# A gated cross-attention block on one core: reordering ScalarE's and GpSimd's work in the first attention group

## The chip, the cores and the metric

The kernel runs on one core of a Trainium2 chip. A core has five engines that each work through their own list of instructions in order: TensorE (PE in the profile, its weight loads PEld), VectorE (DVE), ScalarE (ACT), GpSimd (POOL) and SyncE (SP, which here issues most DMAs). An instruction that must wait for another engine's result holds up all that stands behind it in its own list. The metric is the time of one execution on the device in microseconds (us), as the median of several.

## The reference

The reference is a gated cross-attention layer followed by a gated linear layer, all in fp32:

```
x = x + tanh(g_xattn) * (softmax(q k^T / 8) v) Wo + bo     q = layernorm(x) Wq, k = ctx Wk, v = ctx Wv
x = x + tanh(g_ffn)   * (layernorm(x) W[idx] + b[idx])     idx = argmax(log_softmax(logits) + gumbel(u))
```

There are 4 batches of 2048 tokens with 512 features, 16 heads of 64, and 77 context tokens of 384 features for each batch.

## The kernel before

**Tiling.** The 8192 tokens go through in 16 groups of 512 (`T`, `NGRP`), four groups to a batch. The weights are folded first: a matrix `m` for each batch stands for Wq times that batch's keys, so that scores come from x in one product, and a matrix `vo` stands for values times Wo, so that the attention output comes from the probabilities in one product. `m` and `vo` are built once for all batches, stored to DRAM (`m_d`, `vo_d`), and one batch's part is loaded at a time (`load_m`, `load_vo`).

**Seven products.** Each big product (scores `ps_s`, attention `ps_a`, linear layer `ps_f`) is a two by two block product done with seven block products in place of eight. The class `Seven` (L445) holds this. It needs sums of weight blocks (`weight_sum`, L119, on POOL) and sums of column blocks called T1 to T4 (`Columns.sum`, L434, on POOL). `product(s)` issues the s-th block product on TensorE into one of three PSUM banks r; `post(s)` (L482) moves a result out: by ACT as a copy (`keep`, L472 or L476), or by DVE as an addition to what lies in SBUF already (L491). The order is a table (block, columns, bank r, starts a new bank):

```
ORDER = ((0, "B11", 0, True), (3, "T1", 1, True), (4, "T2", 0, False), (1, "B21", 2, True),
         (5, "T3", 0, False), (6, "B22", 1, False), (2, "T4", 0, False))
```

Blocks 0, 3, 4 and 2 are copied out by ACT, blocks 1, 5 and 6 are added by DVE. A product that goes on in a bank (False) must wait until the post before it has read that bank.

**Order of the work.** It is written out by hand: the program's order is each engine's order, and only the semaphores are put in for it. PSUM has seven banks for all products (`bank`, L82), handed out in turn as they come free.

**The stretch around the change** is the passage from set-up to the steady loop, group 0 (L738 to L800):

- `build_vo(p, engines)` (L327) makes the `vo` rows of the heads 2p and 2p+1. It takes six PSUM banks: for each of three row chunks one matmul for each of the two heads (L336). Each bank is scaled by the gate and copied to SBUF by DVE (L339) or ACT (L341), by the letters of `engines`, which repeat; then SP stores it (L345, L346).
- `head_max` (L527, DVE), `exps(i, n0, n1)` (L533, one ACT instruction for each of 64 pieces, 16 to a head), `head_sum` (L542, a sum and a reciprocal on DVE) and `head_scale` (L547, POOL) make the softmax of one group, head set by head set (four of them).
- `p_columns(i, k0, k1)` (L551) transposes key chunks k0 to k1 on DVE into the tile `pT`, from all four head sets at once. The attention product reads `pT`.
- In the loop at L747 the score products of group 1 (`s0`) alternate with the sets p = 4 to 7 of VO and with the exponentials of group 0. In the loop at L770 the remaining score products of group 1 (`s1` and `s2`) run while the last head sets are summed and scaled and the probabilities transposed; POOL makes T1 of `pT` and three of the four sums of VO (`weight_sum(vo, n)`: n = 0 makes block 5, n = 1 block 3, n = 2 block 4, n = 3 block 6). Then comes the steady loop over the groups (L802), which begins with the attention product `at` of group 0.

At the head of the program (L163 to L187) TensorE runs three matmuls on zeros, ACT and SP issue the first loads, and POOL writes the constants `neghalf` (-0.5) and `ones`. ACT's first computing instruction is then the copy of the first key projection (L275).

Of the kernel before, what the change touches and what calls it, by code (L numbers as in the profile page):

```python
# [8 lines left out]
F32 = mybir.dt.float32  # L9
U32 = mybir.dt.uint32  # L10
AF = mybir.ActivationFunctionType
# [3 lines left out]
P = 128  # L15
# [4 lines left out]
def flamingo_block_kernel(  # L20
# [33 lines left out]
    nc = tc.nc  # L54
    NT, D = x.shape
# [26 lines left out]
    small = ctx.enter_context(tc.tile_pool(name="small", bufs=2))  # L82
# [5 lines left out]
    def bank(name):  # L88
        return pm.tile([P, 512], F32, tag="mm", name=name)
# [8 lines left out]
    vo = cp.tile([P, 7, KH, D // 2], F32, tag="vo")  # L98
# [5 lines left out]
    neghalf = cp.tile([P, NG], F32, tag="neghalf")  # L104
# [9 lines left out]
    def flat(t):  # L114
        n = len(t.shape) - 1
        names = " ".join("abcdef"[:n])
        return t.rearrange(f"p {names} -> p ({names})")

    def weight_sum(w, n, engine=None):  # L119

        to, a, b_, op = ((5, 0, 3, ALU.subtract), (3, 3, 2, ALU.add), (4, 3, 0, ALU.subtract),
                         (6, 1, 4, ALU.subtract))[n]
        (engine or nc.gpsimd).tensor_tensor(flat(w[:, to]), flat(w[:, a]), flat(w[:, b_]), op)
# [19 lines left out]
    t = wp.tile([P, NK * T + KH * T2], F32, tag="pT", name="wq")  # L143
# [41 lines left out]

    nc.gpsimd.memset(neghalf, -0.5)
    nc.gpsimd.memset(ones, 1.0 / D)  # L187

    def by_chunk(t):

        return t.rearrange("p (a q e) -> p q a e", a=NA, e=32)

    def chunked(t):
        return t.rearrange("p (q a e) -> p q a e", a=NA, e=32)
# [61 lines left out]
    def v_cols(p, at, n):  # L256
        return vT_f[:, ds(p * BP + at, n)] if p < 7 else wf_f[:, ds(6 * D + at, n)]
# [65 lines left out]
    def stage_of(h):  # L323

        return vo_st[h if h < 2 else 2 + (h - 2) % (len(vo_st) - 2)]

    def build_vo(p, engines):  # L327
        n = 0
        for c in range(3):
            r = min(P, BP - c * P)  # L330
            for hh in range(2):
                stg = stage_of(2 * p + hh)
                hr = ts(hh, DH)
                ps = bank("ps_vo")

                nc.tensor.matmul(ps, v_cols(p, c * P, P)[hr], wo[hr, p, :], start=True, stop=True)  # L336
                src, dst = by_chunk(ps[:r, :]), chunked(stg[:r, c, :])
                if engines[n % len(engines)] == "D":
                    nc.vector.tensor_scalar(dst, src, tgx[:r], None, ALU.mult)  # L339
                else:  # L340
                    nc.scalar.activation(dst, src, AF.Copy, scale=tgx[:r])  # L341
                n += 1
        for hh in range(2):
            d, stg = vo_d[2 * p + hh], stage_of(2 * p + hh)
            nc.sync.dma_start(out=d[0 : 2 * P].rearrange("(c r) e -> r c e", r=P), in_=stg[:, 0:2])  # L345
            nc.sync.dma_start(out=d[2 * P :], in_=stg[: BP - 2 * P, 2])  # L346
# [5 lines left out]
    def load_vo(bi):  # L352
        src = vo_d.rearrange("h (r b k) e -> (h r) b k e", b=B, k=NK)[:, bi]
        for o, c in ((0, 0), (1, 0), (1, 1), (0, 1)):
            nc.sync.dma_start(out=vo[:, BLK[o, c]], in_=src[:, ts(c, KH), ts(o, D // 2)])
# [161 lines left out]
    def s_rows(i, k, cols):  # L517
        if i not in sc:
            sc[i] = wp.tile([P, HA, NG, JP], F32, tag="s", name="s")
        nc.vector.transpose(key_chunk(sc[i], k), cols.rearrange("p (g h r) -> p g h r", h=HA, r=R))  # L520

    def head(i, h):
        return sc[i][:, h, :, :J]
# [3 lines left out]
    def head_max(i, h):  # L527
        mx = stat[:, ds((16 + h) * NG, NG)]
        nc.vector.tensor_reduce(mx, head(i, h), AX.X, ALU.max)  # L529
        nmx[h] = small.tile([P, NG], F32, tag=f"nmx{h}", name="nmx")  # L530
        nc.vector.tensor_tensor(nmx[h], mx, norms[i].down, ALU.mult)  # L531

    def exps(i, n0, n1):  # L533

        for n in range(n0, n1):
            h, g = n // NG, n % NG
            nc.scalar.activation(head(i, h)[:, g, :], head(i, h)[:, g, :], AF.Exp,  # L537
                                 scale=norms[i].up[:, g : g + 1], bias=nmx[h][:, g : g + 1])
# [3 lines left out]
    def head_sum(i, h):  # L542
        sums[h] = sm = small.tile([P, NG], F32, tag=f"sm{h}", name="sm")
        nc.vector.tensor_reduce(sm, head(i, h), AX.X, ALU.add)  # L544
        nc.vector.reciprocal(sm, sm)  # L545

    def head_scale(i, h):  # L547
        nc.gpsimd.tensor_tensor(head(i, h), head(i, h), sums[h].unsqueeze(2).to_broadcast([P, NG, J]),  # L548
                                ALU.mult)

    def p_columns(i, k0, k1):  # L551
        for k in range(k0, k1):
            if k == 0:
                t = wp.tile([P, NK * T + KH * T2], F32, tag="pT", name="pT")
                pT[i] = Columns(t[:, : NK * T].rearrange("p (n t) -> p n t", t=T),
                                T1=t[:, NK * T :].rearrange("p (n t) -> p n t", t=T2))
            nc.vector.transpose(pT[i].all[:, k, :].rearrange("p (g h r) -> p g h r", h=HA, r=R),  # L557
                                key_chunk(sc[i], k))
# [103 lines left out]
    def centre_wf(wfr, c):  # L662
        nc.gpsimd.tensor_tensor(wfr[:, c, :], wfr[:, c, :], wf_mean, ALU.subtract)
        for o in range(2):
            nc.gpsimd.tensor_scalar(chunked(wf[:, BLK[o, c // 2], c % 2, :]), by_chunk(wfr[:, c, :])[:, ts(o, 2)],
                                    tgf, None, ALU.mult)
# [10 lines left out]
    def norm_step(n, s):  # L677
        if s == 0:
            n.gather()
        elif s == 1:  # L680
            n.calc()
            n.power()
        elif s == 2:
            n.back()
# [61 lines left out]
    e = (8, 16, 24, 32, 41, 50, 57)  # L746
    for s in range(6):  # L747
        s0.product(s)
        s0.post(s)
        if s < 2:  # L750
            centre_wf(wfr, 2 * s)
            centre_wf(wfr, 2 * s + 1)
        if s == 2:
            weight_sum(wf, 0)
            weight_sum(wf, 1)
        if s == 3:
            weight_sum(wf, 2)
        if s < 4:
            build_vo(4 + s, "DDA" if s < 2 else "D")
        if s < 2:  # L760
            head_max(0, 2 + s)
        exps(0, e[s], e[s + 1])
        if s == 3:
            weight_sum(wf, 3)
            load_vo(0)
        if 3 <= s:
            head_sum(0, s - 3)
            head_scale(0, s - 3)
    exps(0, 57, 64)
    for s in range(7):  # L770
        s1.product(s)
        s2.product(s)
        if s == 0:
            s1.post(0)
            s2.post(0)
            s0.product(6)
            s0.post(6)
            head_sum(0, 3)
            head_scale(0, 3)
        if s == 3:  # L780
            norm_step(n1, 2)
        if 1 <= s < 5:
            p_columns(0, (0, 2, 5, 7)[s - 1], (2, 5, 7, 10)[s - 1])
        if s == 2:
            pT[0].sum("T1")
        if s == 3:
            weight_sum(vo, 0)
        if s == 4:
            weight_sum(vo, 1)
        if s == 5:  # L790
            weight_sum(vo, 2)
            for k in range(4):
                s_rows(1, (0, 1, KH, KH + 1)[k], s0.chunk(k // 2, k % 2))
        if 0 < s:
            s1.post(s)
            s2.post(s)
# [5 lines left out]
    for i in range(1, NGRP):  # L802
# [69 lines left out]
        for s in range(7):  # L872
# [12 lines left out]
            if 1 <= s:  # L885
                e = (0, 10, 20, 32, 44, 56, 64)
# [121 lines left out]
    def by_feature(t, h, v):  # L1008

        return t[:, ts(v, NG // 2), ts(h, D // NA // 2)]  # L1010
# [24 lines left out]
    for s in range(6):  # L1035
# [23 lines left out]
        if s == 5:  # L1059
            f_rows(j, ff, 0, 0)  # L1060
            t = by_feature(ts_[j], 0, 0)
# [50 lines left out]
```

## Time and profile before

| what | value |
|---|---|
| time, median of 3 runs | 1245.52 us (1245.17 to 1245.72) |
| the profiled execution: time | 1246.03 us |
| its span in the trace | 1244.2 us |
| PE busy | 99% of the span, 5704 matmul passes |
| PEld busy | 85% |
| DVE busy | 73% |
| POOL busy | 72% |
| ACT busy | 55% |
| granted TensorE clock | 0.998 of full speed |
| share of the chain by `ps_s`, `ps_a`, `ps_f` | 39%, 37%, 15% |

An fp32 matmul shows as two passes, so counts of passes are twice those of matmuls. A line of the timeline has the start in us from the span's start, the length in us, the engine, the line of the program, the operation, the tile written and the tiles read, shapes, the count of instructions merged into the line, and in square brackets the idle time of the engine just before it with what ended it. A line of the chain has the start, the length, and what ran, with the number of merged instructions. A line of the waits has who waited for whom, the total in us, how often, and the longest.

### The profile page before, as it was taken

What the parts mean: (1) busy time and instruction counts of PE and PEld (TensorE: products, weight loads), DVE (VectorE), ACT (ScalarE), POOL (GpSimd) and SP (SyncE); (2) the same over time, 40 slices, a digit from 0 to 9 for tenths busy, and PEclk for the clock granted to TensorE, in tenths of its full rate; (3) what the DMA queues carried; (4) which work ended last, traced back from release to release, by engine and by line L of the source; (5) the groups of instructions that cost most, each with busy time, mean ns of one, the idle gap of its engine ahead of it and who ended that gap; (6) DMA issues with size and microseconds to landing.
All of it is one profiled execution on the core that took longest, in us unless ns stands there. A gap on an engine that the chain in (4) does not pass through costs nothing.

```text
span 1244.2 us, 16997 instructions
## 1 busy us (share of the span) xinstructions
PE 1234.0 (99%) x5704; PEld 1063.7 (85%) x5704; DVE 907.3 (73%) x1850; ACT 683.4 (55%) x1957; POOL 895.4 (72%) x486
## 2 busy tenths in 40 slices
PE   9999999999999999999999999999999999999997
PEld 6686888888888888888888888888888888888886
DVE  6778976666977766677776767776776877666576
ACT  4639545638274563827356382745638274563824
POOL 5558885857957785685968778575976877585766
PEclk9999999999999999999999999999999999999999
DMA  9868200314024030304106030212304121010102
GB/s 268 300 203 274 57 1 1 68 43 111 1 50 103 1 68 1 68 22 112 20 1 153 1 68 2 47 22 85 68 1 111 43 51 18 1 35 1 35 1 67
DMA packets 95221, 80.27 MB, mean 65 GB/s; under 512 B 3856, under 2 KB 83088, under 8 KB 95136
## 3 DMA queue, kind: packets, MB, share of 16 engines
q1 hardware_dynamic: 92496, 76.61, 24.1%
q10 hardware_dynamic: 2032, 1.47, 0.4%
q8 instruction: 45, 0.74, 0.3%
q0 software_dynamic: 608, 1.13, 0.2%
q14 instruction: 40, 0.33, 0.1%
HBM read 44.07 MB, written 35.13 MB: 64 GB/s over the span
## 4 chain that ended last, share of the span: by engine, by line
PE 96%; DVE 2%; ACT 0%; POOL 0%; issue 0%; DVEq 0%
PE ps_s L466 39%; PE ps_a L466 37%; PE ps_f L466 15%; PE ps_kv L270 2%; PE ps_vo L336 2%; PE ps_m L300 1%; DVE s L370 1%; PE ps_w L167 0%; ACT t L591 0%; POOL r L398 0%; DVE t L417 0%; DVE r L393 0%; DVE y L417 0%; DVE snap L491 0%; DVE y L587 0%
## 5 line engine op out<-in xcount | busy, mean ns | idle before, releaser
L466 PE MATMUL ps_a<-pT,vo 128*128 128x256 f32 x2240 | 486.2, 379 | 0.0
L466 PEld LDWEIGHTS ps_a<-pT,vo 128*128 128x128 f32 x2240 | 425.6, 190 | 57.9
L537 ACT ACTIVATE s<-s,nmx,up 128x77 f32<-128x77 f32 x1024 | 355.6, 445 | 0.8 <-DVE nmx L531 0.8
L437 POOL TENSOR_TENSOR pT<-pT 128x1280 f32<-128x1280 f32 x64 | 186.0, 2907 | 171.4 <-PE ps_a L466 161.9
L466 PE MATMUL ps_s<-tq,m 128*128 128x256 f32 x1280 | 290.6, 380 | 0.0
L466 PEld LDWEIGHTS ps_s<-tq,m 128*128 128x128 f32 x1280 | 242.6, 190 | 36.1 <-issue 2.3
L472 ACT COPY snap<-ps_s 128x512 f32<-128x512 f32 (+1 forms) x188 | 93.6, 515 | 292.7 <-DVE t L417 130.5
L466 PE MATMUL ps_s<-xc,m 128*128 128x256 f32 x960 | 221.1, 379 | 0.0
L466 PEld LDWEIGHTS ps_s<-xc,m 128*128 128x128 f32 x960 | 182.2, 190 | 27.3 <-issue 1.2
L548 POOL TENSOR_TENSOR s<-s,sm 128x1232 f32<-128x1232 f32 x64 | 145.2, 2271 | 46.7 <-DVE sm L545 46.7
L491 DVE TENSOR_TENSOR snap<-snap,ps_s 128x512 f32<-128x512 f32 (+1 forms) x141 | 83.7, 594 | 130.1 <-PE ps_s L466 125.0
L466 PE MATMUL ps_f<-tq,wf 128*128 128x256 f32 x512 | 118.3, 379 | 0.0
L557 DVE STREAM_TRANSPOSE pT<-s 128x512 f32<-128x512 f32 x160 | 101.0, 678 | 15.6 <-POOL s L548 15.6
L437 POOL TENSOR_TENSOR tq<-xc,tq 128x512 f32<-128x512 f32 x64 | 85.4, 1335 | 35.5 <-PE ps_f L466 33.0
L398 POOL TENSOR_TENSOR r<-r,neghalf 32x16 f32<-32x16 f32 (+1 forms) x33 | 93.2, 2833 | 21.9 <-DVE r L393 21.3
L466 PEld LDWEIGHTS ps_f<-tq,wf 128*128 128x128 f32 x512 | 97.3, 190 | 13.2
L544 DVE TENSOR_REDUCE sm<-s 128x16 f32<-128x1232 f32 x64 | 91.5, 1430 | 20.7 <-ACT s L537 20.7
L520 DVE STREAM_TRANSPOSE s<-snap 128x512 f32<-128x512 f32 x156 | 99.9, 685 | 6.1 <-ACT snap L472 3.8
L529 DVE TENSOR_REDUCE ps_st<-s 128x16 f32<-128x1232 f32 x64 | 92.4, 1444 | 2.1
L466 PE MATMUL ps_f<-xc,wf 128*128 128x256 f32 x384 | 90.7, 379 | 0.0
L437 POOL TENSOR_TENSOR tq<-xc 128x512 f32<-128x512 f32 x64 | 81.6, 1275 | 7.1 <-DVE xc L412 5.8
L472 ACT COPY snap<-ps_f 128x512 f32<-128x512 f32 x63 | 36.9, 586 | 87.8 <-PE ps_f L466 85.2
(138 smaller groups left out, 1187.0 us busy)
## 6 DMA issues: line engine op xcount, KB each, us to landing
xg<-in_x_dram SPq DMA_DIRECT2D x64, 256.0 KB, 6.0
out_dram<-y SPq DMA_DIRECT2D x60, 256.0 KB, 4.1
vo<-vo_d SPq DMA_DIRECT2D x16, 640.0 KB, 6.4
m<-m_d SPq DMA_DIRECT2D x12, 640.0 KB, 4.2
vo_d<-vo SPq DMA_DIRECT2D x14, 512.0 KB, 3.3
m_d<-vo SPq DMA_DIRECT2D x4, 960.0 KB, 5.0
wq<-in_WqT_dram SPq DMA_DIRECT2D x8, 256.0 KB, 6.5
wq<-in_Wo_dram SPq DMA_DIRECT2D x1, 2048.0 KB, 13.8
```

The source lines that it names most:

```text
L270: nc.tensor.matmul(ps[:, :n], w[:, c, ts(p, P)], keys[:, c].rearrange("p b j -> p (b j)"), start=(c == 0), stop=(c == NCC - 1))
L398: nc.gpsimd.tensor_tensor(r, r, neghalf[:32, : r.shape[1]], ALU.pow)
L437: (engine or nc.gpsimd).tensor_tensor(self.at[name], self.at[a], self.at[b_], op)
L466: nc.tensor.matmul(self.ps[r][:, n, :], self.w(blk, c, pair), self.cols(cname, c), start=(first and n == 0 and c == 0), stop=(c == h - 1), ...
L472: nc.scalar.copy(dst, self.ps[r])
L491: nc.vector.tensor_tensor(c, c, self.ps[r], ALU.add)
L520: nc.vector.transpose(key_chunk(sc[i], k), cols.rearrange("p (g h r) -> p g h r", h=HA, r=R))
L529: nc.vector.tensor_reduce(mx, head(i, h), AX.X, ALU.max)
L537: nc.scalar.activation(head(i, h)[:, g, :], head(i, h)[:, g, :], AF.Exp, scale=norms[i].up[:, g : g + 1], bias=nmx[h][:, g : g + 1])
L544: nc.vector.tensor_reduce(sm, head(i, h), AX.X, ALU.add)
L548: nc.gpsimd.tensor_tensor(head(i, h), head(i, h), sums[h].unsqueeze(2).to_broadcast([P, NG, J]), ALU.mult)
L557: nc.vector.transpose(pT[i].all[:, k, :].rearrange("p (g h r) -> p g h r", h=HA, r=R), key_chunk(sc[i], k))
```

## The change

Four edits, all in set-up and group 0:

1. After the constants are written, ACT computes one exponential of one column of `neghalf` into a small tile (tag `sm0`) that nothing reads.
2. For p = 6 and p = 7 (s = 2 and 3) the third of VO's six banks is copied by ACT rather than DVE ("DDADDD" for "D").
3. At s = 3 two of the exponentials are issued ahead of `build_vo(7)`, so that ACT's copy for p = 7 stands behind them. The last three exponentials (61 to 63) of group 0 are issued after the three copies that ACT makes in the first step of the next loop (`s1.post(0)`, `s2.post(0)`, `s0.post(6)`), not ahead of them.
4. `weight_sum(vo, 0)` on POOL moves from s = 3, behind T1 of `pT`, to s = 1, ahead of it.

ACT gains three instructions in all (1957 by the page before), DVE loses two, and POOL, PE and SP have as many as before. The table loads on ACT stay three, at the same three places in its list.

```diff
     nc.gpsimd.memset(neghalf, -0.5)
     nc.gpsimd.memset(ones, 1.0 / D)
+    t = small.tile([P, 1], F32, tag="sm0", name="sm")
+    nc.scalar.activation(t, neghalf[:, 0:1], AF.Exp)
...
+        e0 = e[s]
+        if s == 3:
+            exps(0, e0, e0 + 2)
+            e0 += 2
         if s < 4:
-            build_vo(4 + s, "DDA" if s < 2 else "D")
+            build_vo(4 + s, "DDA" if s < 2 else "DDADDD")
         if s < 2:
             head_max(0, 2 + s)
-        exps(0, e[s], e[s + 1])
+        exps(0, e0, e[s + 1])
         if s == 3:
             weight_sum(wf, 3)
             load_vo(0)
         if 3 <= s:
             head_sum(0, s - 3)
             head_scale(0, s - 3)
-    exps(0, 57, 64)
+    exps(0, 57, 61)
     for s in range(7):
         s1.product(s)
         s2.product(s)
...
             s0.product(6)
             s0.post(6)
+            exps(0, 61, 64)
             head_sum(0, 3)
             head_scale(0, 3)
+        if s == 1:
+            weight_sum(vo, 0)
         if s == 3:
             norm_step(n1, 2)
         if 1 <= s < 5:
             p_columns(0, (0, 2, 5, 7)[s - 1], (2, 5, 7, 10)[s - 1])
         if s == 2:
             pT[0].sum("T1")
-        if s == 3:
-            weight_sum(vo, 0)
         if s == 4:
             weight_sum(vo, 1)
```

## The prediction

> **What bounds the kernel now.** I read four views: the page, TensorE's waits, the chain, and the timeline from 85 to 140 us, the one stretch that the diff touches apart from the first instructions.
>
> The page, engines' busy time:
> ```profile
> PE 1234.0 (99%) x5704; PEld 1063.7 (85%) x5704; DVE 907.3 (73%) x1850; ACT 683.4 (55%) x1957; POOL 895.4 (72%) x486
> ```
> The waits of TensorE:
> ```profile
> PE ps_w L167 <- DVE tq L163: 1.5, 1, 1.5
> ```
> The chain, as start, length, what:
> ```profile
> 1.45 5.49 PE ps_w L167 x6
> ...
> 78.95 0.86 PE ps_w L659 x2
> ...
> 89.30 2.77 PE ps_vo L336 x12
> ...
> 98.70 3.02 PE ps_vo L336 x12
> ...
> 103.64 3.08 PE ps_vo L336 x12
> ...
> 108.64 3.02 PE ps_vo L336 x12
> 111.66 23.51 PE ps_s L466 x108
> ```
> PE is busy 1234.0 of 1244.2 us, and its only listed wait is the first instruction. In the stretch, the one loss that the chain shows is that the last three sets of VO banks (p = 5, 6, 7) take 3.02, 3.08 and 3.02 where an undisturbed one takes 2.77: 0.25 + 0.31 + 0.25 = 0.81 us. So a reordering can win at most that here, and it loses whatever idle time it opens on PE.
>
> The timeline, as start, length, engine, line:
> ```profile
> 101.68 1.27 ACT L341 ACTIVATE vo<-ps_vo,tg 128x512 f32<-128x512 f32 x2
> ...
> 102.84 2.86 ACT L537 ACTIVATE s<-s,nmx,up 128x77 f32<-128x77 f32 x8
> ...
> 105.57 0.59 ACT L472 COPY snap<-ps_s 128x512 f32<-128x512 f32 x1
> ...
> 106.04 13.83 ACT L537 ACTIVATE s<-s,nmx,up 128x77 f32<-128x77 f32 x40
> ...
> 109.74 4.03 DVE L339 TENSOR_SCALAR vo<-ps_vo,tg 128x512 f32<-128x512 f32 x6 [0.31 <-PE ps_vo L336]
> ...
> 115.53 8.95 POOL L548 TENSOR_TENSOR s<-s,sm 128x1232 f32<-128x1232 f32 x4 [2.45 <-DVE sm L545]
> ...
> 119.74 0.59 ACT L472 COPY sn<-ps_s 128x512 f32<-128x512 f32 x1
> ...
> 119.90 1.44 DVE L544 TENSOR_REDUCE sm<-s 128x16 f32<-128x1232 f32 x1 [0.16 <-ACT s L537]
> 120.21 0.88 ACT L472 COPY snap<-ps_s 128x256 f32<-128x256 f32 x2
> 121.37 0.25 DVE L545 RECIPROCAL sm<-sm 128x16 f32<-128x16 f32 x1
> ...
> 124.51 4.27 DVE L557 STREAM_TRANSPOSE pT<-s 128x512 f32<-128x512 f32 x7 [2.89 <-POOL s L548]
> ...
> 127.68 2.92 POOL L437 TENSOR_TENSOR pT<-pT 128x1280 f32<-128x1280 f32 x1 [3.20 <-DVE pT L557]
> ...
> 131.41 0.65 DVE L491 TENSOR_TENSOR sn<-sn,ps_s 128x512 f32<-128x512 f32 x1
> ...
> 132.42 2.75 PE L466 MATMUL ps_s<-tq,m 128*128 128x256 f32 x12
> ```
> Here is a second chain, a hair behind PE. ACT runs 40 exponentials without a pause from 106.04; the last ends at 119.87 and releases DVE's last row sum (119.90), its reciprocal (to 121.62), POOL's fourth head_scale (to 124.48), and DVE's ten transposes into pT (from 124.51). Behind those in DVE's queue stands s1.post(4), the addition at 131.41, which ends at 132.06. By the order table, s1.product(6) ("T4", bank 0) accumulates into the bank that s1.post(4) ("22", bank 0) reads, so it must wait for it. PE starts it at 132.42. The slack of the whole chain is 0.36 us.
>
> **The change part by part.**
>
> *Head exponential.* One ACT instruction of about 0.2 us after the first table load (2.21 to 3.49). Its input, POOL's memset at 0.80, is long written. ACT then idles until 8.59, 5.09 us waiting for PE: that is the cover. The instruction listing has three table loads before and after, so none is saved or added. Cost 0; were there one more load (1.28), the cover would still hold it. The page "ScalarE: Activation LUTs", section "What ACT_TABLE_LOAD costs", adds a drain of 1.38 us to a load, 2.66 in all; this trace shows only the 1.28, and the sum is 0 either way.
>
> *Two banks from DVE to ACT (third of six, p = 6 and 7).* DVE sheds two copies of 4.03/6 = 0.67. That gives PE nothing: the sixth matmul of a set waits for the bank that the first copy (still DVE's, at the same time) gives back, so 3.08 and 3.02 stay. Bounds: 0 to a win of 0.31 + 0.25 = 0.56; I take 0. SP's stores of these two sets and the vo load behind them (117.43) can only leave earlier. ACT's full queue takes the two copies, at (102.84 - 101.68)/2 = 0.58 each.
>
> ACT anew: the first copy runs at 106.04; ten exponentials at 13.70/40 = 0.343 each end at about 110.05. The second copy needs its bank of p = 7: the first bank is ready at 109.74 (DVE waited 0.31 for it), the next pair one PE step later, 2.77/3 = 0.92 at most, so at about 110.6. ACT waits 0.55 (bounds 0 and 0.61). Then copy, 27 exponentials (9.25), and the queue reaches the snap copies at 120.45 instead of 119.74.
>
> *Last three exponentials behind three copies.* The copies take 119.74 to 121.09, 1.2 us of queue (0.12 overlaps what follows). So the last exponential ends later by 0.58 + 0.58 + 0.55 + 1.2 = 2.9 us: at 122.8, not 119.87. Queued behind it: nothing that PE needs soon. The copies themselves are 0.7 late, but s1.product(2), which needs the first, starts at 122.05 (132.42 less 48 passes of 0.216, the pace of 28.49 us for 132 in a later stage of the chain) against its end at 121.05: hidden.
>
> *Down the second chain.* Sum and reciprocal take 119.90 to 121.62 = 1.72: done at 124.55. POOL's fourth head_scale used to wait for POOL itself until 122.2, so 0.4 of the delay is absorbed; it now starts 0.15 after the reciprocal (115.53 against 115.40 at the first) and ends at 126.97. The transposes start at 127.0 instead of 124.51: 2.5 late, on a DVE that idles meanwhile and is then full. s1.post(4) ends 7.55 later (132.06 - 124.51): 134.55.
>
> *VO's first sum ahead of T1.* One POOL instruction of 2.9 us goes in front of T1, in the 3.20 us that POOL idles there. Its vo blocks were loaded from 117.43 and land some 6.4 later (median of these loads), before 126.97. It ends at 129.95, T1's inputs (five transposes, 0.6 each) are there at 130.0, so T1 is not held up; the other two sums end at about 139.4 instead of 139.88. No cost, and no PE wait was there to win.
>
> *Sum.* s1.product(6) can start at 134.55 plus hand-over and an unhidden weight load. Bounds for that: 0.05 and 0.05 + 0.22; I take 0.15. So 134.7 against 132.42: PE idles 2.3 us. Everything behind it is gapless PE work, so 2.3 reaches the end. The rest of DVE's and ACT's queue (head_max, the next exponentials) is 2.5 late against a PE that is 2.3 late; the next consumer, the fifth attend product, had 2.7 us in hand (ACT's copy before it ended at 149.55, and PE, 80 passes of 0.216 after 135.01, reached it at 152.3). Bounds of the sum: 1.7 (no wait for the bank, the shortest restart) and 2.9 (copies at their full 0.69 and 1.35, the longest restart).
>
> The profiled execution took 1246.03 (span 1244.2 and 1.8 around it), 0.5 above the median 1245.52. In its terms the changed kernel takes 1248.3; against the median, 1245.52 + 2.3 = **1247.8 us**.
>
> **The clock.** Right after the start six ps_w passes take 5.49 us (0.92 each); at 78.95 two of the same shape take 0.86 (0.43 each): TensorE starts at about half speed, and those first 5.3 us cost 5.49 - 6 x 0.43 = 2.9. No row shows an idle PE of 2.3 us in mid-run, so a second slow spell is bounded by 0 and 2.9; I take 0, since PE never stood still that long after the start. The page "TensorE: Matmul & The Clock Gate", section "Why this matters for your kernels", sets the limit at idle gaps of about 3 us; by it the sum stays 2.3, and a gap past it would make it about 5.2.
>
> **Rivals.**
> 1. *Not slower: the second chain does not reach PE.* It decides at 124.87, the latest start of the transposes that keeps 0.36 of slack. For it: PE waits nowhere now. Against: ACT has no idle time between 101 and 121, so 2.9 of added queue can't vanish. Were it hidden, and the 0.56 won, 1245.0 to 1245.5.
> 2. *Slower by more than 2.5: the idle gap costs clock as well.* 2.3 plus up to 2.9: 1248.5 to 1250.7. For it: the slow start. Against: no such row in mid-run.
> 3. *A second late wait:* the delay breaks another slack, first the fifth attend product, which waits for ACT's copy behind twenty exponentials. Price up to 1 us: 1248.8. Against: 2.7 us in hand and only 0.2 of relative delay.
> 4. *The change does what it seems meant to:* ACT's copies earlier, PE's split pairs closed, 1245.0. Against: the copies come later, not earlier.
>
> **How the numbers follow.** My forecast 80%, rivals 1 and 4 together 9%, rival 2 6%, rival 3 5%. The forecast's own range is 1247.2 to 1248.4; the range that holds 8 in 10 widens it by half a microsecond below and above for the spread of runs (1245.17 to 1245.72) and for rival 3: 1246.5 to 1249.0. A difference of 0.2% (2.5 us) is about what a measurement of this kernel can tell from none; that line lies at 1248.0, inside my bounds: some three tenths of the forecast's 80%, and rivals 2 and 3, lie past it. So slower 0.36, same 0.62; faster by 2.5 us would need gains that PE's 0.81 us do not hold: 0.02.
>
> **What would show it.** In the changed profile TensorE's waits list a second line, ps_s on DVE's sn addition, of about 2.3 us near 132; the last exponential ends near 122.8, the transposes start near 127.0, ps_vo of p = 6 and 7 still takes 3.08 and 3.02, and PE is gapless from there on. I am wrong if PE shows no such wait, if the transposes start before 124.9, or if the clock row drops after the gap.

## The result, and the profile after

| what | before | after |
|---|---|---|
| time, median of 11 runs each | 1245.52 us (1244.76 to 1246.36) | 1248.53 us (1247.80 to 1249.42) |
| the profiled execution: time | 1246.03 us | 1249.04 us |
| its span | 1244.2 us | 1247.3 us |
| idle time of PE in mid-run | none | 2.00 us, once |

The ratio of the medians is 1.0024, with a 95% interval from 1.0016 to 1.0032. The kernel became slower by 3.0 us. The prediction said 1247.8 us, in a range from 1246.5 to 1249.0.

In these pages the profiled execution of the changed kernel runs 0.92 us ahead of the one of before from the first products on: its six `ps_w` passes at the start take 4.41 us where they took 5.49. This differs from one execution to the next of the same program: in three profiles of the changed kernel these passes take 4.41, 4.56 and 5.15 us. So the edits are not taken to be its cause, and 0.92 is added below wherever a time of after is held against one of before or of the prediction. Line numbers of after are two higher than before's up to L760.

The page of the changed kernel, engines' busy time:

```profile
PE 1235.0 (99%) x5704; PEld 1064.3 (85%) x5704; DVE 905.9 (73%) x1848; ACT 684.5 (55%) x1960; POOL 894.8 (72%) x486
```

It hardly differs: DVE gave up two instructions, ACT got three, and PE does the same passes in 1.0 us more of busy time. The shares tell nothing of what happened. The waits of TensorE in the changed kernel (who waited for whom, total in us, how often, longest):

```profile
PE ps_s L468 <- DVE sn L493: 2.0, 1, 2.0
PE ps_w L167 <- DVE tq L163: 1.5, 1, 1.5
```

The second line is the old one. The first is new, and it is the only wait that the change put into PE's list of 5704 passes. The chain of the changed kernel, in the stretch from 95 to 140 us, shows what it waits for (start, length, what):

```profile
107.73 1.97 PE ps_vo L338 x8
109.69 0.67 ACT vo L343
110.36 6.68 ACT s L539 x20
...
117.11 2.50 ACT s L539 x7
119.61 0.47 ACT sn L474
120.07 0.75 ACT snap L474 x2
120.82 1.05 ACT s L539 x3
...
121.89 1.45 DVE sm L546
...
123.36 0.26 DVE sm L547
...
123.77 2.27 POOL s L550
...
126.06 2.21 DVE pT L559 x4
...
133.04 0.58 DVE sn L493
...
133.67 4.54 PE ps_s L468 x12
138.21 1.94 PE ps_a L468 x9
```

Before, the chain went through PE alone here. Now it leaves PE at 109.7, when the matmul for a bank of p = 7 releases ACT's copy of it. It follows ACT's exponentials, the three copies that now stand in front of the last three, the row sum and reciprocal, the fourth `head_scale` and the transposes, and it comes back to PE at 133.67 with `s1.product(6)`. Every piece that the prediction called the second chain is in it.

The last lines hold a second thing. The twelve passes of `s1.product(6)` take 4.54 us where before they took 2.75. The stretches of the changed kernel show why (from and to, length, then busy us and number of instructions of PE, PEld, DVE, ACT and POOL, the granted TensorE clock as a share of full speed, the DMA share and GB/s):

```profile
4.65:131.67 127.02, 127.02 (x593) 91.42 (x591) 97.38 (x240) 74.37 (x213) 82.24 (x64) 1.00 0.87 263
131.67:133.67 2.00, 0.00 (x1) 0.00 (x1) 2.00 (x5) 0.00 (x0) 2.00 (x4) 1.00 0.00 0
133.67:134.36 0.69, 0.69 (x3) 0.64 (x4) 0.69 (x2) 0.00 (x0) 0.69 (x1) 1.00 0.00 0
134.36:137.77 3.41, 3.41 (x10) 2.70 (x9) 3.41 (x7) 0.58 (x1) 3.33 (x2) 0.50 0.00 0
137.77:150.00 12.23, 12.23 (x58) 10.75 (x58) 11.89 (x19) 7.74 (x22) 8.04 (x4) 1.00 0.00 1
```

PE stands still from 131.67 to 133.67 while DVE and POOL are busy throughout. It then works for 0.69 us at full clock, and at 134.36 the granted clock falls to 0.50 for 3.41 us. The attention product starts at these times in the changed kernel, in before, and in a second execution of the changed kernel that has no drop of the clock (below):

```profile
138.05 7.29 PE L468 MATMUL ps_a<-pT,vo 128*128 128x256 f32 x33
```

```profile
135.01 30.38 PE L466 MATMUL ps_a<-pT,vo 128*128 128x256 f32 x140
```

```profile
136.88 8.37 PE L468 MATMUL ps_a<-pT,vo 128*128 128x256 f32 x38
```

The stretch between two starts, of `s1.product(6)` and of the attention product, is 138.05 - 133.67 = 4.38 us here and was 135.01 - 132.42 = 2.59. Of the 1.79 more, 0.10 is the restart (the execution without the drop takes 134.19 to 136.88, which is 2.69), and 1.69 is the clock.

The sum of the profiled execution: 0.92 gained at the start; 2.17 lost in the gap, as `s1.product(6)` starts at 133.67 + 0.92 = 134.59 in place of 132.42 (the wait is listed with 2.00, since the pass before it still counts as busy for the other 0.17); 0.10 lost by the restart; 1.69 lost by the clock. Together it is 3.04 us later. The spans differ by 1247.27 - 1244.25 = 3.02. Nothing else moved the end.

### The profile page after: what moved, and what is told of

It is laid out like the page before. It is cut to its first block, busy times and chain, and to the rows that moved or that the text cites. A ratio compares the mean times of both kernels' runs of the same rounds, so it can differ in the third digit from the quotient of the medians.

```text
span 1247.3 us, 16995 instructions
## 1 busy us (share of the span) xinstructions
PE 1235.0 (99%) x5704; PEld 1064.3 (85%) x5704; DVE 905.9 (73%) x1848; ACT 684.5 (55%) x1960; POOL 894.8 (72%) x486
## 4 chain that ended last, share of the span: by engine, by line
PE 94%; DVE 3%; ACT 1%; POOL 0%; issue 0%; DVEq 0%; POOLq 0%
PE ps_s L468 37%; PE ps_a L468 37%; PE ps_f L468 15%; PE ps_kv L272 2%; PE ps_vo L338 2%; PE ps_m L302 1%; ACT s L539 1%; DVE s L372 1%; DVE pT L559 0%; ACT t L593 0%; PE ps_w L167 0%; POOL r L400 0%; DVE snap L493 0%; DVE t L419 0%; DVE r L395 0%
```

## Experiments

Four theories of the parts were put up before the runs: that the second chain, made late by edits 2 and 3 (the banks and the split), causes the gap; that only one of them does; that the head exponential or VO's sum has a part in it; and, on the clock, that a gap of this kind lowers it afterwards. The diffs below are against the changed kernel unless said otherwise.

### The split undone

```
-    exps(0, 57, 61)
+    exps(0, 57, 64)
...
-            exps(0, 61, 64)
```

> The changed kernel with the last three exponentials back in front of ScalarE's three copies; the head exponential, the two banks on ScalarE and VO's first sum stay. Theory A (the second chain: last exponential, row sum, head_scale, transposes, s1.post(4), s1.product(6)): ScalarE's delay is 0.58 + 0.58 + 0.45 = 1.6 us, less 0.4 of slack on GpSimd and 0.36 before TensorE, plus 0.15 to restart: an idle gap of 0.8 to 1.1 us, the clock stays at 1.00, 1246.3 to 1246.7 us. Theory B (the two banks on ScalarE do no harm, the split alone does all of it): no gap, 1245.5. Theory C (any idle gap of TensorE costs one 3.41 us spell at half clock, 1.7 us): 1248.2.

Measured: 1247.06 us (1246.04 to 1247.56), against 1245.51 for before on the same chip, ratio 1.0011 (1.0002 to 1.002). The wait of TensorE and the copy from which ACT's queue can be timed, in this kernel:

```profile
PE ps_s L468 <- DVE sn L493: 0.7, 1, 0.7
```

```profile
110.43 0.69 ACT L343 ACTIVATE vo<-ps_vo,tg 128x512 f32<-128x512 f32 x1 [0.39 <-PE ps_vo L338]
111.02 10.40 ACT L539 ACTIVATE s<-s,nmx,up 128x77 f32<-128x77 f32 x30
```

The last exponential now ends 121.42 - 110.43 = 10.99 us after the start of that copy; in the changed kernel it is 121.86 - 109.68 = 12.18. So the split is worth 1.19 us of lateness; the prediction had 1.2. Of the gap 0.66 is left (0.93 with the restart and the end of the pass before), and the clock stays at 1.00 after it. So the gap doesn't come from the split alone.

### The two banks given back to DVE

```
-            build_vo(4 + s, "DDA" if s < 2 else "DDADDD")
+            build_vo(4 + s, "DDA" if s < 2 else "D")
```

> The changed kernel with the six banks of p = 6 and 7 all on VectorE again; the split of the last exponentials and the rest stay. Theory A: ScalarE's delay is 1.2 us, less 0.4 and 0.36, plus 0.15: a gap of 0.5 to 0.7 us, clock 1.00, 1246.0 to 1246.3 us. Theory B turned round (the banks alone do it): no gap, 1245.5. Theory C: 0.6 and 1.7 more, 1247.8.

Measured: 1246.64 us (1245.69 to 1247.27), ratio 1.0007 (0.9998 to 1.0016). The wait:

```profile
PE ps_s L468 <- DVE sn L493: 0.5, 1, 0.5
```

Each edit alone costs PE less than a microsecond (0.93 and, here, 0.79, in both with the restart and the end of the pass before), and both together 2.27. The lateness of the last exponential adds up, nearly, and the loss does not. ACT's copy that starts at 105.57 in before starts at 105.42 with the banks alone, 105.33 with the split alone and 104.65 with both. Moved by these differences, the last exponential ends 1.70, 1.41 and 2.91 us after the 119.87 of before. Taking off the prediction's slack of 0.36 and its 0.4 of absorption on POOL, and putting on 0.10 for the restart, gives 1.04, 0.75 and 2.25. The slack of the one chain is spent once, and the second edit pays nearly in full. Both edits make the gap.

The times of both runs lie above the ranges expected, and 0.3 to 0.6 above before plus the time lost in the gap of their profile. Of the 0.6 of the split undone, 0.15 has a row: the 32 passes of score products that start at 117.74 in before take 7.07 us there, and 7.22 here, where ACT's first copy ends only at 121.89. The rest is within the intervals and left as unexplained.

### Only the head exponential and VO's sum

Against before, this kernel has the new exponential at the head and VO's first sum ahead of T1, and nothing else of the change.

```
+    t = small.tile([P, 1], F32, tag="sm0", name="sm")
+    nc.scalar.activation(t, neghalf[:, 0:1], AF.Exp)
...
+        if s == 1:
+            weight_sum(vo, 0)
...
-        if s == 3:
-            weight_sum(vo, 0)
```

> The kernel before with only the head exponential and VO's first sum ahead of T1. Theory A: neither touches a chain that TensorE waits on: no gap, 1245.5 us within 0.3. Rival D (the head exponential shifts the start of the program, or the sum on GpSimd slows the transposes beside it): some 0.3 to 1 us either way, and a transposes row longer than 4.27 us for seven.

Measured: 1245.90 us (1245.13 to 1246.50), ratio 1.0001 (0.9992 to 1.001). TensorE's only wait is the old one at the start. The timeline of this kernel:

```profile
3.51 0.20 ACT L189 ACTIVATE sm<-neghalf 128x1 f32<-128x1 f32 x1
8.06 0.42 ACT L277 COPY wf<-ps_kv 128x308 f32<-128x308 f32 x1 [4.34 <-PE ps_kv L272]
...
123.92 2.91 POOL L123 TENSOR_TENSOR vo<-vo 128x1280 f32<-128x1280 f32 x1
...
127.16 2.92 POOL L439 TENSOR_TENSOR pT<-pT 128x1280 f32<-128x1280 f32 x1 [0.33 <-DVE pT L559]
```

The exponential takes 0.20 us, and ACT idles 4.34 us behind it for PE. VO's sum runs in the time in which POOL waited for the transposes, and T1 still waits for DVE (0.33), not for the sum. The seven transposes beside VO's sum take 4.27 us, as in before, so rival D has no row for it. Two edits of the four open no wait. The median lies 0.4 above before, 0.1 more than was expected, and the interval holds zero: neither a cost nor a win can be told.

### The two posts issued ahead of the transposes

If the gap comes from the order of DVE's queue, where `s1.post(4)` stands behind transposes that start late, it must vanish when the posts of s = 3 and 4 are issued first.

```
+        if 3 <= s < 5:
+            s1.post(s)
+            s2.post(s)
         if 1 <= s < 5:
-            p_columns(0, (0, 2, 5, 7)[s - 1], (2, 5, 7, 10)[s - 1])
+            p_columns(0, (0, 2, 5, 5)[s - 1], (2, 5, 5, 10)[s - 1])
...
-        if 0 < s:
+        if 0 < s and s not in (3, 4):
             s1.post(s)
             s2.post(s)
```

> The changed kernel in full, but VectorE takes the posts of s = 3 and s = 4 (s1.post(3), s2.post(3), s1.post(4), s2.post(4)) ahead of the transposes of key chunks 5 to 9. ScalarE's late exponentials stay, so the transposes still start near 126. Theory A (the wait is made by VectorE's queue order): s1.post(4) ends near 130, TensorE has no wait at s1.product(6), no slow spell, 1245.5 us within 0.4. Rival E (the late transposes themselves hold up the attention product that reads them): a gap at the first ps_a products instead, 1246.5 or more.

Measured: 1247.60 us (1246.71 to 1248.15), ratio 1.0014 (1.0005 to 1.0023). The wait at `s1.product(6)` is gone, as expected, but the time of before does not come back, against the 1245.5 expected. The transposes start as late as in the changed kernel (127.17, with a start of this execution that is 0.15 later than before's, against 126.06 + 0.92 = 126.98), and `s1.post(4)` now stands ahead of the second half of them:

```profile
127.17 3.08 DVE L559 STREAM_TRANSPOSE pT<-s 128x512 f32<-128x512 f32 x5 [2.45 <-POOL s L550]
...
131.08 0.67 DVE L493 TENSOR_TENSOR sn<-sn,ps_s 128x512 f32<-128x512 f32 x1
```

The waits of TensorE:

```profile
PE ps_w L167 <- DVE tq L163: 1.5, 1, 1.5
PE ps_f L468 <- POOL tq L439: 1.4, 1, 1.4
```

No wait stands at the first attention products, where rival E put one. A new wait stands 36 us later, at the first linear-layer product of the loop (`ff.product(1)`, "T1"), for a column sum on POOL. POOL's timeline there, in this kernel and then in before:

```profile
154.59 2.27 POOL L550 TENSOR_TENSOR s<-s,sm 128x1232 f32<-128x1232 f32 x1 [3.25 <-DVE sm L547]
...
163.88 2.27 POOL L550 TENSOR_TENSOR s<-s,sm 128x1232 f32<-128x1232 f32 x1 [1.99 <-DVE sm L547]
...
167.46 1.27 POOL L439 TENSOR_TENSOR tq<-xc 128x512 f32<-128x512 f32 x1
```

```profile
151.79 2.27 POOL L548 TENSOR_TENSOR s<-s,sm 128x1232 f32<-128x1232 f32 x1 [0.42 <-DVE sm L545]
...
161.03 2.27 POOL L548 TENSOR_TENSOR s<-s,sm 128x1232 f32<-128x1232 f32 x1 [1.98 <-DVE sm L545]
...
164.60 1.27 POOL L437 TENSOR_TENSOR tq<-xc 128x512 f32<-128x512 f32 x1
```

The softmax of the next group is late too: its first scaling 2.80 us, its third 2.85, and behind that in POOL's queue the sum that PE needs, 2.86 (0.15 of this is the start of the execution, by which PE is late too). In before PE reached `ff.product(1)` at 166.95, 1.08 us after that sum was done (164.60 + 1.27). So that much lay in hand, and the rest of the delay became a wait of 1.35. In the changed kernel this wait isn't there; PE itself is late by then.

Two things follow. The cause of the gap at `s1.product(6)` is the place of `s1.post(4)` in DVE's queue: with the same late transposes and the post ahead of them, it is gone. And curing one consumer doesn't buy back the time, since the lateness goes on to the next group: DVE's transposes and the row maxima behind them are late, ACT's next ten exponentials start at 143.96 where they started at 141.15, and the next consumers had little in hand. The fifth attention product, which waits for an ACT copy, is only just touched (two passes from 152.22 take 0.76 us, in before two from 151.84 take 0.59), and `ff.product(1)`, with its 1.1 us, pays the rest.

### Ten exponentials behind the copies in place of three

```
-        exps(0, e0, e[s + 1])
+        exps(0, e0, min(e[s + 1], 54))
...
-    exps(0, 57, 61)
...
-            exps(0, 61, 64)
+            exps(0, 54, 64)
```

> The changed kernel with ten exponentials (54 to 63) behind ScalarE's three copies in place of three. Each one more behind them delays the last by 0.343: 7 x 0.343 = 2.4 us. Theory A: the gap at s1.product(6) grows by that, from 2.0 idle (2.27 lost) to 4.4 idle (4.67 lost). Theory F (the clock halves for one spell of 3.41 us, at 1.7 us, when one of the fixed windows of 3.41 us holds enough idle time, wherever it lies): a gap of 4.4 always fills enough of a window, so the profile has at least one spell at 0.5 right behind it, and every execution pays 1.7: 1245.5 + 4.7 + 1.7 = 1251.9 us, up to 1253.6 with two spells. Theory G (the spell seen behind the gap was chance): 1250.2.

Measured: 1250.54 us (1250.05 to 1251.07), against 1245.42 for before on the same chip, ratio 1.004 (1.0026 to 1.0055). The gap is 2.90 us, not the 4.4 expected. Its timeline on ACT shows what was wrong with that figure:

```profile
110.09 0.69 ACT L343 ACTIVATE vo<-ps_vo,tg 128x512 f32<-128x512 f32 x1 [0.44 <-PE ps_vo L338]
110.67 6.95 ACT L539 ACTIVATE s<-s,nmx,up 128x77 f32<-128x77 f32 x20
117.52 0.57 ACT L474 COPY sn<-ps_s 128x512 f32<-128x512 f32 x1
117.99 0.37 ACT L474 COPY snap<-ps_s 128x256 f32<-128x256 f32 x1
119.17 0.58 ACT L474 COPY snap<-ps_s 128x512 f32<-128x512 f32 x1 [0.80 <-PE ps_s L468]
119.65 3.53 ACT L539 ACTIVATE s<-s,nmx,up 128x77 f32<-128x77 f32 x10
```

What stands in front of the last exponential is the same whether three or ten exponentials follow the copies: all the exponentials and three copies. Its end depends on how long ACT idles before the copies, and here they come so early that PE has not made the third bank yet (0.80). That wait and 0.1 around it are the whole difference: 2.00 + 0.9 = 2.9. The direction of the expectation held, its size was a slip in counting the queue.

On the clock, the stretches of this kernel:

```profile
132.08:134.98 2.90, 0.00 (x1) 0.01 (x1) 2.90 (x7) 0.00 (x0) 2.90 (x4) 1.00 0.01 2
134.98:135.60 0.62, 0.62 (x3) 0.57 (x4) 0.62 (x2) 0.00 (x0) 0.62 (x1) 1.00 0.00 0
135.60:139.02 3.42, 3.42 (x10) 2.71 (x9) 3.42 (x7) 0.59 (x1) 3.34 (x2) 0.50 0.00 0
```

The drop came again, of the same length and depth, after a longer gap. The sum 1245.42 + 2.90 + 0.27 + 1.69 gives 1250.3 against the 1250.5 measured (0.27 are the end of the pass before and the restart, as above).

### Five behind the copies, and the changed kernel itself twice more

To see whether the drop belongs to the gap or to the execution, the changed kernel was profiled twice more, beside a kernel with five exponentials behind the copies.

```
-    exps(0, 57, 61)
+    exps(0, 57, 59)
...
-            exps(0, 61, 64)
+            exps(0, 59, 64)
```

> The changed kernel with five exponentials (59 to 63) behind the three copies in place of three: 2 x 0.343 = 0.7 more, a gap of 2.7 idle, 2.95 lost. Theory F: a spell at half clock in most executions (the gap fills two windows evenly only in a few), 1248.5 without it and 1250.2 with it.

> The changed kernel itself, for another profiled execution. Theory A: the wait on VectorE's sn addition, 1.9 to 2.2 us idle, in every one. Theory F: whether the spell at half clock follows depends on where the windows lie, counted in steps of 3.41 us from the first change of the clock: a spell when the gap lies within one window, none when a window's edge cuts it near its middle. About 1249.2 with it, 1248.2 without.

> The same once more. Theory A: the same wait. Theory F: as in the run before this one, a spell or none by the place of the gap in the windows.

All three show the same gap of 2.00 us. For the five this is not the 2.7 expected, by the same slip as above: PE is ahead of the copies here, so the last exponential ends no later than with three. It took 1247.97 us and shows no drop. The two executions of the changed kernel took 1247.89 and 1249.04 us. The first has no drop, its stretches around the gap:

```profile
131.90:134.19 2.29, 0.29 (x2) 0.00 (x1) 2.29 (x5) 0.00 (x0) 2.29 (x4) 1.00 0.00 1
134.19:138.70 4.51, 4.51 (x21) 4.01 (x22) 4.51 (x9) 0.96 (x2) 4.43 (x2) 1.00 0.00 0
```

The second has it, in the same view cut at the same places of the program:

```profile
131.30:133.61 2.31, 0.31 (x3) 0.01 (x1) 2.31 (x5) 0.00 (x0) 2.31 (x4) 1.00 0.00 0
133.61:138.15 4.54, 4.54 (x13) 3.72 (x14) 4.54 (x9) 0.59 (x2) 4.46 (x2) 0.62 0.00 0
```

The program, the chip and the gap are the same. In the 4.5 us after the gap one execution does 21 passes and the other 13; eight passes of 0.216 are 1.73 us. So the drop is not a property of the gap's length alone. What differs is where the gap lies in the clock's own rhythm. The first record of the clock at full speed, called the release here, stands at 4.65, 4.95 and 5.90 us in the three executions with a drop (the view counts the time before the first record as 1.00, though the `ps_w` passes there run at about half speed). The clock falls 129.71 us after the release in each of them, which is 38 times 3.413. Counting steps of 3.413 us from the first release gives:

| execution | clock released at | idle stretch of PE | idle time within one step | drop |
|---|---|---|---|---|
| changed kernel, first profile | 4.65 | 131.67 to 133.67 | 2.00 | 134.36 to 137.77 |
| changed kernel, third | 4.95 | 131.61 to 133.61 | 2.00 | 134.65 to 138.06 |
| ten behind | 5.90 | 132.08 to 134.98 | 2.78 | 135.60 to 139.02 |
| changed kernel, second | 6.13 | 132.19 to 134.19 | 1.76 | none |
| five behind | 6.25 | 132.25 to 134.25 | 1.70 | none |
| posts first | 6.64 | 1.35 us at 168.8 | at most 1.35 | none |
| split undone | 6.29 | 0.66 us at 133.2 | at most 0.66 | none |
| banks given back | 6.41 | 0.52 us at 132.9 | at most 0.52 | none |

In these eight executions the clock falls at the end of a step in which PE idled 2.0 us or more, and does not where it idled 1.76 or less. That a step ends at the edge that cuts the gap in the second execution (132.43) is a count from the release, since no row marks it there.

The ends of the traces put the count to a second test, since PE runs out of work there. The steps in which it does so, counted from the same releases, in the changed kernel's first profile and with the split undone:

```profile
1236.86:1240.28 3.42, 1.59 (x8) 1.05 (x6) 3.27 (x7) 2.22 (x10) 3.17 (x3) 1.00 0.01 2
1240.28:1243.69 3.41, 0.00 (x0) 0.00 (x0) 1.39 (x2) 0.00 (x0) 1.36 (x2) 1.00 0.89 203
```

```profile
1235.09:1238.51 3.42, 1.34 (x7) 0.83 (x5) 3.25 (x8) 1.98 (x9) 3.08 (x4) 1.00 0.07 16
1238.51:1241.92 3.41, 0.00 (x0) 0.00 (x0) 1.16 (x2) 0.00 (x0) 1.19 (x1) 0.50 0.90 200
```

PE idles 1.83 us of the first step in the one, and the clock stays at 1.00 through the next; it idles 2.08 in the other, and the clock falls at the step's end. All ten traces of this case agree: after a last working step with 1.06, 1.12, 1.39, 1.76 or 1.83 us of idle time the clock stays (and falls after the next step, which is idle throughout), as it does after 0.26 in before, and after one with 2.08, 2.19, 2.54 or 3.18 it falls. The fall comes a whole number of steps after the release in each, in the second execution of the changed kernel too (362 steps of 3.413, at 1241.75). So the line lies between 1.83 and 2.00 us of idle time in one step. A kernel with a gap set to either side of it on purpose was not tried.

## Why the prediction was right, and where it was not

**The head exponential at 0: right.** It takes 0.20 us in front of 4.34 us of idle time. The Trainium skill's page "ScalarE: Activation LUTs", section "What ACT_TABLE_LOAD costs", was weighed with its drain of 1.38 us. The load takes 1.28 here, and the exponential starts at 3.51, 0.01 after its end; no run here shows the drain.

**The two banks: right.** DVE's relief gave PE nothing: the sets of p = 6 and 7 cost what they did. Their rows are 3.15 and 3.09 us long in the timeline of after, as in before. On ACT the banks made the last exponential 1.7 us late (predicted 0.58 + 0.58 + 0.55), with a wait of 0.44 for the bank of p = 7 in place of 0.55.

**The three copies: right.** 1.2 predicted, 1.19 measured by undoing the split.

**Down the second chain: right to a few hundredths.** Some of that closeness is luck, as the 0.15 taken between the reciprocal and `head_scale` is 0.13 by the rows that it cites, and was 0.15 in the changed kernel; the path and its one slack are not. The starts and ends in the timeline of the changed kernel:

| step | predicted, us | measured + 0.92, us |
|---|---|---|
| last exponential ends | 122.8 | 122.78 |
| transposes start | 127.0 | 126.98 |
| `s1.post(4)` ends | 134.55 | 134.53 |
| PE restarts, with the unhidden weight load | 134.7 | 134.69 |
| lost in the gap | 2.3 | 2.27 |

**VO's sum ahead of T1 at 0: right.** It fills POOL's wait, and T1 waits for DVE as before.

**The clock term: wrong, and the only one that moved the time off the forecast.** The prediction put a second slow spell between 0 and 2.9 us and took 0, on the ground that PE never stood still that long after the start. That holds for mid-run only: at its end the trace of before has one step with PE idle throughout (1235.72 to 1239.13), and the clock falls behind it. The term measured 1.69 us in the profiled execution, 1.60 and 0 in the two others. The Trainium skill's page "TensorE: Matmul & The Clock Gate", section "Why this matters for your kernels", sets the limit at idle gaps of about 3 us; here 2.00 us was enough in two executions of three. The same page, in "What's actually happening", gives a free-running window of 3413 ns; the 3.41 us of each drop and the 129.71 us from release to drop agree with that. By the measured line, between 1.83 and 2.00 us, a gap is enough that takes up 59% of one such window, and 54% is not. A drop of the clock after the gap was among the prediction's own signs of being wrong, and it came. Rival 2, to which the prediction gave 6%, is what a part of the executions do: 1249.04 lies inside its 1248.5 to 1250.7.

The median is 1248.53 - 1247.8 = 0.73 us above the forecast. It lies outside the forecast's own 1247.2 to 1248.4 and inside the wider range. That it stayed inside is in part luck: a drop of 1.69 in every execution would have made 1245.52 + 2.27 + 1.69 = 1249.5. Which of the runs without a profile had a drop is not shown. The four slowest of the 11, 1249.01 to 1249.42 us, have mean granted clocks of 0.996 and 0.997, and the other seven, 1247.80 to 1248.66, of 0.998. If those four are the ones with a drop, the median execution has none, and its 0.73 must come from elsewhere. The start of the execution fits: the drops go with early releases, and the executions with a release at 4.65 and 4.95 had gained 0.5 to 0.6 us at the start against the one at 6.13. So the spared executions are those that start late. As an estimate, the slower half of before's runs (1245.52 to 1246.36) plus 2.27 makes 1247.8 to 1248.6, close to the seven. An early release has two sides here: it wins up to 0.6 at the start, and loses 1.6 to 1.7 later.

**The slack behind the gap: right in effect, incomplete in place.** The prediction named the fifth attention product, with 2.7 us in hand, as the next consumer. Nothing further waits in the changed kernel, so rival 3 did not happen. With the gap taken away that product is just touched, and the wait comes at the linear layer's `ff.product(1)`, where only 1.08 us lay in hand. The working had followed ACT's copies and left out what goes through POOL.

**Rival 1** (the chain stays hidden) falls by the new wait line, and **rival 4** by the copies: the first of them starts at 119.50 + 0.92 = 120.42, later than the 119.74 of before.

## What to carry to other kernels

When one engine is gapless, look for the chain with the least slack beside it, here 0.36 us, and follow every move of work along it before asking what the move relieves: relief on an engine that nobody waits for is worth nothing, and two small delays on one chain share one slack. Ask also what comes next once that chain is late, for the delay goes on to the next group and meets the next slack. A gap on TensorE can cost more than its own length: in these runs 2 us of idle time could take 1.7 us more through the clock, in some executions and not in others, so a gap near that size is best priced with both ends, and two or three profiles tell more than one.

## What was not expected of the hardware

A gap of 2.00 us lowered the granted clock to 0.50 for 3.41 us, and it did so 0.69 and 1.04 us after PE had started again, not at the start of the work. The same program with the same gap did it in two of three profiled executions. It goes with the idle time that falls into one step of 3.413 us counted from the first release: 2.00 and 2.78 did it in mid-run and 2.08 at the end of a run, and 1.83, 1.76 and 1.70 did not.
